# A two-layer block on one core: Du/dt in a stream of its own, new TensorE durations for the planner, products of the identity in the first sample, and a bias loaded earlier

## The chip, the core and the metric

The kernel runs on one core of one Trainium2 chip. Its engines are TensorE (PE: matrix products, with PEld for the loads of their stationary operand), VectorE (DVE), ScalarE (ACT), GpSimd (POOL) and SyncE (SP, which here only issues DMAs). The metric is device time in microseconds; lower is better. Before the change the median of three runs is 2807.39 us (2804.79 to 2811.74).

## What is computed

Sixteen samples of 256 tokens by 256 features, float32 throughout. Each `_L...` is a function of the reference; the indices and masks are left out here.

```python
def reference(x, ...):
    # layer 0
    x = x + attn0(cross(x, fside, embed[itok]))   # softmax(q k^T) v, then causal attention, 16 heads of 16, rotary
    x = x + ffn0(x @ W[cat] + b[cat])             # gate/up/down with FP4-like quantization of inputs and weights
    # layer 1
    du = zX * lap_x(x) + zY * lap_y(x) + zR * x * (1 - x)
    x = x + attn1(rmsnorm(du) * g)                # 16 heads of 64, segments of 128, 16 learned keys in front
    x = x + mixture(conditioned(x))               # 8 experts, top 2, and a shared one
    return x
```

The line `du` (Du/dt in what follows) is three pointwise terms: second differences along both axes, the one along the tokens made as a product with a 256x256 matrix, and a reaction term. attn1 reads nothing else.

## The kernel before

The program has two parts. `woven` does everything up to the second attention, sample by sample, and leaves each sample's x in DRAM; `mixture` then does the experts over all samples. The change touches `woven` alone.

`woven` is written as generators, called streams, each yielding one instruction at a time. `stage_a` loads a sample, does the cross attention, the projection to heads and the row maxima of the first attention's scores; `stage_e` does its exponentials, values and output projection and sets `done["A"]`. `stage_gate`, `stage_up` and `stage_down` quantize and transpose the three weights of the feed forward, once, at the start. `stage_f` is the feed forward (`done["F"]`). `stage_p` loads the constants of the second attention, then for each sample computes Du/dt and its normalized transpose zT (`diffuse`), and the projections of four groups of four heads (`project4`). `stage_g` takes the scores and the softmax of a group (`scores4`), `stage_v` its values and the output projection (`values4`), and after a sample's last group stores x.

`weave` interleaves the streams while the program is built, so that the order on each engine is fixed before anything runs. It keeps a planned time for each engine, from durations that `Unit.cost` gives, and a planned time at which each tile is written and read. In each step it looks at the next instruction of every stream, and issues the one that could start first; ties go to the stream that stands first in the list. A stream that didn't issue the last TensorE instruction is charged `TURN` (0.1 us). A DMA's data counts as there `LANDING` (4.5 us) after its issue. A yielded function is a gate: its stream waits until it returns true. A yielded `Want` asks for a free PSUM buffer; there are two pairs of banks and four single banks (`g.singles`) for all streams.

The engines then run their fixed orders. An instruction that waits holds up all that stands behind it on its engine; SP's DMAs too are issued in order, one after another.

At the start SP issues, in this order: the first sample's xT, fT, the embedding row, fside and x (`fetch_a`), then wqkv, bqkv, three small tables, the output bias `bout`, `wout0`, and the first pieces of the three feed forward weights. GpSimd's first work is x + bout, then the query `a_qT`; TensorE's first products are the scores of the cross attention from `a_qT`, and VectorE's `a_stat` takes their row maxima.

`diffuse` is part of `stage_p`: for sample b it is yielded after the four projections of sample b - 1, and the projections of b come behind it. The tile zT has one buffer. `project4` loads `wq`, `wv` and the rows `wo` of the output projection; `wo` is read by `values4` at the end of the group and has three buffers.

All helpers that record instructions do it in one line (160 before), so groups of the profile are told apart by tiles.

Of the kernel before, what the change touches and what calls it, by code (L numbers as in the profile page):

```python
# [12 lines left out]
F32 = mybir.dt.float32  # L13
# [6 lines left out]
P = 128  # L20
S = 256
D = 256
H = 16
DH0 = 16
DH1 = 64
# [91 lines left out]
class Op:  # L117


    def __init__(self, choices, outs, ins):  # L120
        self.choices, self.outs, self.ins = choices, outs, ins

# [1 line left out]
HOP = 0.15  # L126
LANDING = 4.5
TURN = 0.1


def is_ap(x):
# [3 lines left out]
def row_size(ap):  # L135
    return math.prod(ap.shape[1:])
# [9 lines left out]
class Unit:  # L146
# [17 lines left out]
    def cost(self, fn, outs, ins):  # L164
        if self.name == "SP":
            return 0.06
        if self.name == "PE":
            if fn == "transpose":
                return 0.15
            lhsT, rhs = ins  # L170
            fp32 = 4 if rhs.dtype == F32 else 1
            rows, cols, n = lhsT.shape[0], row_size(lhsT), row_size(rhs)
            side = (2 if rows <= 32 else 1) * (3 if cols <= 32 else 2 if cols <= 64 else 1)
            return max((2 if fp32 == 4 else 1) * cols / 2070, fp32 * n / 2070 / side) + 0.01
        fixed, each = COSTS[self.name]
        n = max(row_size(x) for x in outs[:1] + ins)
        if fn == "reciprocal":
            each = 0.006
        return fixed + each * n + (0.3 if len(outs) > 1 else 0)


def weave(streams):

    free, written, read, rings = {}, {}, {}, {}
    turn = None
    names = lambda aps: [x.tensor.name for x in aps]

    def ready(op, engine):
        t = 0.0
        for n in names(op.ins):
            when, by = written.get(n, (0.0, engine))
            t = max(t, when + (HOP if by != engine else 0.0))
        for x in op.outs:
            n = x.tensor.name
            before = [written.get(n), read.get(n)]
            ring = rings.get(getattr(x.tensor, "tag", None), [])
            if n not in ring and ring:  # L200
                bufs = x.tensor.bufs or x.tensor.tag_meta.bufs
                if len(ring) >= bufs:
                    before += [written.get(ring[-bufs]), read.get(ring[-bufs])]
            for p in before:
                if p and not p[1] == engine == "SP":
                    t = max(t, p[0] + (HOP if p[1] != engine else 0.0))
        return t

    def issue(op, choice, start):
        engine, cost, call = choice  # L210
        free[engine] = start + cost
        end = start + cost + (LANDING if engine == "SP" else 0.0)
        for n in names(op.ins):
            if end > read.get(n, (0.0, engine))[0]:
                read[n] = (end, engine)
        for x in op.outs:
            n, tag = x.tensor.name, getattr(x.tensor, "tag", None)
            written[n] = (end, engine)
            if tag is not None and n not in rings.setdefault(tag, []):
                rings[tag].append(n)  # L220
        call()

    def least(want):

        return min(want.free, key=lambda x: ready(Op([], [x], []), "PE"))


    waiting = [[s, None, None] for s in streams]
    while waiting:
        best, moved = None, False  # L230
        for rank, w in enumerate(waiting):
            while w[1] is None or (callable(w[1]) and w[1]()):
                moved = True
                try:
                    w[1], w[2] = w[0].send(w[2]), None
                except StopIteration:
                    w[0] = None
                    break
            if w[0] is None or callable(w[1]):
                continue  # L240
            if isinstance(w[1], Want):
                if not w[1].free:
                    continue
                op = Op([("PE", 0.0, None)], [least(w[1])], w[1].ins)
            else:
                op = w[1]
            for c in op.choices:
                start = max(ready(op, c[0]), free.get(c[0], 0.0))
                if c[0] == "PE" and w is not turn:
                    start += TURN  # L250
                key = (start, rank, c[1])
                if best is None or key < best[0]:
                    best = (key, w, c, start)
        waiting = [w for w in waiting if w[0] is not None]
        if best is not None:
            _, w, c, start = best
            if isinstance(w[1], Want):
                w[2] = least(w[1])
                w[1].free.remove(w[2])
            else:  # L260
                issue(w[1], c, start)
                if c[0] == "PE":
                    turn = w
            w[1] = None
        else:
            assert moved, "all streams wait"
# [25 lines left out]
def woven(k):  # L292
    nc, tc = k.nc, k.tc
    with ExitStack() as ctx:
        g = Stages()
        g.k, g.a, g.B, g.ident = k, k.a, k.B, k.ident
        g.pe, g.dve, g.act = Unit("PE", nc.tensor), Unit("DVE", nc.vector), Unit("ACT", nc.scalar)
        g.pool, g.sp = Unit("POOL", nc.gpsimd), Unit("SP", nc.sync)
        pool = lambda name, bufs, **kw: ctx.enter_context(tc.tile_pool(name=name, bufs=bufs, **kw))
        g.w = pool("w", 1)  # L300
        g.xp = pool("x", 5)
        g.a_, g.f_, g.l_ = pool("sa", 1), pool("sf", 1), pool("sl", 1)
        space = bass.MemoryType.PSUM
        psum = pool("psum", 1, space=space)
        g.pairs = [psum.tile([P, 2, 512], F32, name=f"pair{i}") for i in range(PAIRS)]
        g.singles = [psum.tile([P, 512], F32, name=f"single{i}") for i in range(8 - 2 * PAIRS)]
        g.live, g.kT = {}, {}
        g.x, g.io, g.done = {}, {}, {"W": 0, "A": 0, "M": 0, "E": 0, "F": 0, "P": 0, "G": 0, "V": 0, "L": 0}
        with tc.manual_schedule():
            weave([stage_a(g), stage_e(g), stage_gate(g), stage_up(g), stage_down(g), stage_f(g), stage_g(g), stage_p(g), stage_v(g)])  # L310


def load(g, pool, name, shape, src):
# [27 lines left out]
def stage_a(g):  # L341
    k, a = g.k, g.a
    yield from fetch_a(g, 0)
    g.wqkv, op = load(g, g.w, "wqkv0", [P, 2, 3 * D], a["w_qkv0"])
    yield op
    g.bqkv, op = load(g, g.w, "bqkv0", [P, 3 * D], a["L0_attn_b_qkv"].unsqueeze(0).to_broadcast([P, 3 * D]))
    yield op
    for name in ("cos0", "sin0", "nsin0"):
        t, op = load(g, g.w, name, [P, 2, DH0 // 2], a[name])
        setattr(g, name, t)  # L350
        yield op
    g.bout, op = load(g, g.w, "bout0", [P, D], a["L0_attn_b_out"].unsqueeze(0).to_broadcast([P, D]))
    yield op
    g.wout0, op = load(g, g.w, "wout0", [P, 2, D], a["w_out0"])
    yield op

# [356 lines left out]
def stage_gate(g):  # L713

    g.gateT = g.w.tile([P, 2, FF0], F32, name="gateT")
    raw = lambda: g.f_.tile([P, 2, D], F32, name="raw", tag="wide", bufs=3)
    yield from quant_rows(g, "L0_ffn_w_gate", g.gateT, raw, None)
    g.done["W"] += 1


def stage_up(g):

    g.upT = g.w.tile([P, 2, FF0], F32, name="upT")
    scratch = scratch_l(g, ("f_pT", "f_pT"), "up")
    yield from quant_rows(g, "L0_ffn_w_up", g.upT, lambda: tile_l(g, [P, 2, D], "f_v", 3), scratch)
    g.done["W"] += 1
# [71 lines left out]
def stage_p(g):  # L798
    k, a = g.k, g.a
# [48 lines left out]
        g.keys.append(t)  # L848
    g.mhalf = g.w.tile([P, 2], F32, name="mhalf")
    yield g.pool.memset(g.mhalf, -0.5)  # L850
    for b in range(g.B):
        yield lambda b=b: g.done["F"] > b
        zT = yield from diffuse(g, b)
        for n in range(4):
            yield lambda i=4 * b + n: i < g.done["V"] + 3
            g.live[4 * b + n] = yield from project4(g, n, zT)
            g.done["P"] += 1


def diffuse(g, b):  # L860
# [21 lines left out]
    yield g.pool.tensor_tensor(ms, ms, g.mhalf, ALU.pow)  # L882
    for st in range(2):
        yield g.dve.tensor_scalar(u[:, st, :], u[:, st, :], ms[:, st : st + 1], None, ALU.mult)
    zT = tile_l(g, [P, 2, S], "e_zT")
    one = yield from single(g, u)
    pt = one.rearrange("p (c t) -> p c t", c=2)
    for c in range(2):
# [8 lines left out]
def project4(g, n, zT):  # L897

    a = g.a
    wq = tile_l(g, [P, 2, 2, 2 * P], "wq", 2)  # L900
    for which in range(2):
        cols = slice((8 * which + 2 * n) * P, (8 * which + 2 * n + 2) * P)
        yield g.sp.dma_start(out=wq[:, which], in_=a["w_qk1"][:, :, cols])
    wv, wo = tile_l(g, [P, 2, 4 * DH1], "wv", 2), tile_l(g, [P, 2, D], "wo", 3)
    yield g.sp.dma_start(out=wv, in_=a["w_v1"][:, :, n * 4 * DH1 : (n + 1) * 4 * DH1])
    yield g.sp.dma_start(out=wo, in_=a["w_out1"][:, 2 * n : 2 * n + 2, :])
    q = tile_l(g, [P, 2, S], "f_q", 3)
    by_seg = lambda t: t.rearrange("p (s t) -> p s t", s=2)
    for which in range(2):
# [16 lines left out]
        yield from mm_(g, pv[:, st, :], [(zT[:, c, st * P : (st + 1) * P], wv[:, c, :]) for c in range(2)])  # L926
    yield copy_(g, v, pv)
    g.singles.append(one)
    return q, v, wo

# [19 lines left out]
            g.done["L"] = b + 1  # L952


def scores4(g, n, q, v, wo):

    keys = g.keys[n]
    prob = tile_l(g, [P, 2, 4, PM + P], "f_prob", 2)
    if n % 2 == 0:
        g.pm = tile_l(g, [P, 2, 8, PM], "f_pm", 2)  # L960
# [566 lines left out]
```

## Time and profile before

| | us |
|---|---|
| median of three runs | 2807.39 |
| the profiled execution | 2814.07 |
| its span | 2812.4 |
| TensorE busy | 2700.6 |
| VectorE busy | 1440.4 |
| ScalarE busy | 927.8 |
| GpSimd busy | 874.7 |
| TensorE's first product starts | 19.53 |
| last part (`mixture`) begins, about | 1820 |

The times of engines are from one execution, taken by the hardware profiler; durations of single instructions come from it too. Its own time, 2814.07 us, is what its span is held against. In the list of groups a line reads: source line, engine, operation, output<-inputs by tile name, partitions x elements and count, then the busy time in us and the mean of one in ns, then the idle time of the engine just before these instructions with what ended it. A product of two float32 operands appears as two records. Matmuls overlap, so the mean of one is longer than busy time divided by count. "PEclk" is the clock that TensorE was granted, as a share of full speed. A table by stretch gives for each: its length, then the busy time and number of instructions of PE, PEld, DVE, ACT and POOL, then PEclk, the share of DMA and its GB/s.

### The profile page before, as it was taken

What the parts mean: (1) busy time and instruction counts of PE and PEld (TensorE: products, weight loads), DVE (VectorE), ACT (ScalarE), POOL (GpSimd) and SP (SyncE); (2) the same over time, 40 slices, a digit from 0 to 9 for tenths busy, and PEclk for the clock granted to TensorE, in tenths of its full rate; (3) what the DMA queues carried; (4) which work ended last, traced back from release to release, by engine and by line L of the source; (5) the groups of instructions that cost most, each with busy time, mean ns of one, the idle gap of its engine ahead of it and who ended that gap; (6) DMA issues with size and microseconds to landing.
All of it is one profiled execution on the core that took longest, in us unless ns stands there. A gap on an engine that the chain in (4) does not pass through costs nothing. (4 is left out here: it accounts for less than half of the span.)

```text
span 2812.4 us, 41924 instructions
## 1 busy us (share of the span) xinstructions
PE 2700.6 (96%) x15819; PEld 2034.8 (72%) x15819; DVE 1440.4 (51%) x3117; ACT 927.8 (33%) x2414; POOL 874.7 (31%) x1030
## 2 busy tenths in 40 slices
PE   5899999999999999999999998799999999999999
PEld 3667777777777777777777777655566888888866
DVE  6456766776776776776777666424340000000023
ACT  2223433334333334334434333323322222222221
POOL 4333433434434444444444343322330000000035
PEclk7789999999999999999999999899999999999999
DMA  3122221222222221231231232241112355555523
GB/s 112 57 83 76 66 84 38 93 79 64 91 90 63 87 94 55 90 96 59 88 97 39 79 94 68 65 141 46 51 38 77 126 189 196 197 197 196 197 83 105
DMA packets 196525, 270.38 MB, mean 96 GB/s; under 512 B 34912, under 2 KB 167264, under 8 KB 186976
## 3 DMA queue, kind: packets, MB, share of 16 engines
q1 hardware_dynamic: 190176, 250.87, 28.0%
q0 software_dynamic: 6144, 16.79, 2.0%
q8 instruction: 127, 2.08, 0.3%
q14 instruction: 78, 0.64, 0.1%
HBM read 207.05 MB, written 60.56 MB: 95 GB/s over the span
## 5 line engine op out<-in xcount | busy, mean ns | idle before, releaser
L160 ACT ACTIVATE f_prob<-pair,f_stat 128x144 f32<-128x144 f32 x512 | 191.2, 379 | 274.1 <-DVE f_stat L160 266.4
L160 DVE TENSOR_TENSOR pair<-pair,mask 128x256 f32<-128x256 f32 (+1 forms) x384 | 198.8, 518 | 132.9 <-PE pair L160 91.9
L1166 POOL DMA_INDIRECT got<-osort,pos_o x64 | 62.2, 972 | 628.2 <-PE bank L49 585.7
L160 PE MATMUL single<-e_zT,wq 128*128 128x256 f32 x1024 | 251.5, 389 | 2.8 <-DMA wq<-in_w_qk 1.4
L1148 ACT ACTIVATE ehT<-bank,own_b 128x256 f32<-128x256 f32 x280 | 132.9, 475 | 348.7 <-PE bank L49 348.7
L49 PE MATMUL bank<-ysT,w 128*128 128x256 f32 x1120 | 247.5, 379 | 0.2 <-ACT ysT L113 0.2
L49 PE MATMUL bank<-w,ehT 128*128 128x256 f32 x1120 | 247.5, 379 | 0.0
L49 PEld LDWEIGHTS bank<-ysT,w 128*128 128x128 f32 x1120 | 212.7, 190 | 29.4 <-ACT ysT L113 0.5
L49 PEld LDWEIGHTS bank<-w,ehT 128*128 128x128 f32 x1120 | 210.2, 190 | 27.2
L160 PEld LDWEIGHTS single<-e_zT,wq 128*128 128x128 f32 x1024 | 188.7, 192 | 39.0 <-DVE pair L160 3.3
L160 PE MATMUL pair<-keys,f_q 32*128 32x144 f32 x2048 | 162.0, 297 | 0.0
L160 PEld LDWEIGHTS pair<-keys,f_q 32*128 32x128 f32 x2048 | 134.2, 187 | 35.8 <-issue 25.2
L160 POOL TENSOR_TENSOR f_q<-f_t,f_t 128x256 f32<-128x256 f32 x128 | 91.6, 736 | 205.6 <-DVE f_t L160 201.0
L160 DVE TENSOR_TENSOR x<-x,single 128x512 f32<-128x512 f32 (+1 forms) x112 | 67.8, 605 | 161.6 <-PE single L160 157.0
L160 POOL TENSOR_SCALAR_AFFINE_SELECT b_e<-b_e 128x512 f32<-128x512 f32 x128 | 83.2, 650 | 207.0 <-ACT b_e L160 206.4
L160 ACT ACTIVATE b_e<-pair 128x768 f32<-128x768 f32 x128 | 103.7, 811 | 132.7 <-PE pair L160 106.1
L160 POOL TENSOR_TENSOR keys<-f_t,f_t 128x256 f32<-128x256 f32 x128 | 93.2, 741 | 167.5 <-DVE f_t L160 166.4
L1156 DVE TENSOR_TENSOR eo<-bank,eb 128x512 f32<-128x512 f32 x35 | 24.2, 692 | 234.4 <-PE bank L49 234.4
L160 PE MATMUL single<-wo,f_oT 128*128 128x256 f32 x512 | 131.6, 390 | 9.1 <-ACT f_oT L160 7.5
L160 DVE TENSOR_REDUCE qpad<-pair 128x2 f32<-128x256 f32 (+1 forms) x256 | 131.0, 554 | 4.4
L160 PE MATMUL pair<-b_qS,b_qkT 17*128 17x256 f32 (+1 forms) x1024 | 123.3, 363 | 5.7 <-DVE qpad L160 2.3
L160 PE MATMUL pair<-b_qkT 16*128 16x128 f32 (+1 forms) x1024 | 126.8, 368 | 1.9 <-ACT b_qkT L160 1.6
(289 smaller groups left out, 5238.5 us busy)
## 6 DMA issues: line engine op xcount, KB each, us to landing
w<-in_w SPq DMA_DIRECT2D x70, 1024.0 KB
ysort<-zero SPq DMA_DIRECT2D x32, 1024.0 KB
wq<-in_w_qk SPq DMA_DIRECT2D x128, 256.0 KB
wv<-in_w_v SPq DMA_DIRECT2D x64, 256.0 KB
wo<-in_w_out SPq DMA_DIRECT2D x64, 256.0 KB
ys<-ysort SPq DMA_DIRECT2D x35, 256.0 KB
osort<-eo SPq DMA_DIRECT2D x35, 256.0 KB
eb<-in_b SPq DMA_DIRECT2D x35, 128.0 KB
```

Of the source, the lines that this page charges most:

```text
L49: nc.tensor.matmul(out, lhsT, rhs, start=start and i == 0, stop=stop and i == last)
L160: return Op([(self.name, self.cost(fn, outs, aps), lambda: call(*args, **kw))], outs, aps)
L1148: nc.scalar.activation(hT[:, f, :], ph, AF.Gelu_apprx_tanh, bias=b1[:, f : f + 1])
L1156: nc.vector.tensor_tensor(o, po, b2.unsqueeze(1).to_broadcast([P, 2, D]), ALU.add)
L1166: nc.gpsimd.indirect_dma_start(out=g, out_offset=None, in_=k.osort[:, :], in_offset=bass.IndirectOffsetOnAxis(ap=r.pos_o[:, i, t : t + 1], ...
```

## The change

It has four parts.

1. `bout` is loaded right behind the first sample's x, ahead of wqkv.
2. The durations that the planner has for TensorE are replaced.
3. A stream `stage_fill` issues products of the identity with itself, 128x128, into a single bank that it keeps for the purpose, until the first sample's attention is done. Nobody reads them. The planner adds `GAP` (0.6 us) to their start when it compares, so that one is taken only where no stream could start anything within 0.6 us of it.
4. `diffuse` moves from `stage_p` to a stream of its own, `stage_d`, which may be a sample ahead of the projections: it starts sample b once its feed forward is done and the projections of b - 2 are recorded. zT gets two buffers. `wo` is loaded in `scores4` instead of `project4`, with two buffers instead of three.

```diff
@@ the planner
+GAP = 0.6
...
             if fn == "transpose":
-                return 0.15
+                return 0.12
             lhsT, rhs = ins
-            fp32 = 4 if rhs.dtype == F32 else 1
-            rows, cols, n = lhsT.shape[0], row_size(lhsT), row_size(rhs)
-            side = (2 if rows <= 32 else 1) * (3 if cols <= 32 else 2 if cols <= 64 else 1)
-            return max((2 if fp32 == 4 else 1) * cols / 2070, fp32 * n / 2070 / side) + 0.01
+            rows, cols, t = lhsT.shape[0], row_size(lhsT), row_size(rhs) / 570
+
+            if rows <= 64:
+                return max(0.155 if rows <= 32 else 0.19, t / 2)
+            return max(t / 3.5, 0.08) if cols <= 32 else max(t / 2, 0.13) if cols <= 64 else t
...
-                key = (start, rank, c[1])
+                key = (start + (GAP if op.filler else 0.0), rank, c[1])
...
-                if c[0] == "PE":
+                if c[0] == "PE" and not w[1].filler:
                     turn = w
@@ woven
-            weave([stage_a(g), stage_e(g), stage_gate(g), stage_up(g), stage_down(g), stage_f(g), stage_g(g), stage_p(g), stage_v(g)])
+            weave([stage_a(g), stage_e(g), stage_gate(g), stage_up(g), stage_down(g), stage_f(g), stage_g(g), stage_p(g), stage_d(g), stage_v(g), stage_fill(g)])
+
+
+def stage_fill(g):
+
+
+    one = g.singles.pop()
+    while g.done["A"] < 1:
+        op = g.pe.matmul(one[:, :P], g.ident, g.ident, start=True, stop=True)
+        op.filler = True
+        yield op
+    g.singles.append(one)
@@ stage_a
     yield from fetch_a(g, 0)
+    g.bout, op = load(g, g.w, "bout0", [P, D], a["L0_attn_b_out"].unsqueeze(0).to_broadcast([P, D]))
+    yield op
     g.wqkv, op = load(g, g.w, "wqkv0", [P, 2, 3 * D], a["w_qkv0"])
...
-    g.bout, op = load(g, g.w, "bout0", [P, D], a["L0_attn_b_out"].unsqueeze(0).to_broadcast([P, D]))
-    yield op
@@ stage_p and stage_d
+    g.done["Z"] = 1
     for b in range(g.B):
-        yield lambda b=b: g.done["F"] > b
-        zT = yield from diffuse(g, b)
+        yield lambda b=b: g.done["D"] > b
+        zT = g.zT.pop(b)
...
+def stage_d(g):
+
+    yield lambda: g.done["Z"]
+    for b in range(g.B):
+        yield lambda b=b: g.done["F"] > b and g.done["P"] >= 4 * b - 4
+        g.zT[b] = yield from diffuse(g, b)
+        g.done["D"] = b + 1
@@ diffuse, project4, scores4
-    zT = tile_l(g, [P, 2, S], "e_zT")
+    zT = tile_l(g, [P, 2, S], "e_zT", 2)
...
-    wv, wo = tile_l(g, [P, 2, 4 * DH1], "wv", 2), tile_l(g, [P, 2, D], "wo", 3)
+    wv = tile_l(g, [P, 2, 4 * DH1], "wv", 2)
...
-    yield g.sp.dma_start(out=wo, in_=a["w_out1"][:, 2 * n : 2 * n + 2, :])
...
-def scores4(g, n, q, v, wo):
+def scores4(g, n, q, v):
...
+    wo = tile_l(g, [P, 2, D], "wo", 2)
+    yield g.sp.dma_start(out=wo, in_=g.a["w_out1"][:, 2 * n : 2 * n + 2, :])
```

Apart from the 90 products of the identity that the planner finds room for, each engine has the same work as before; only ScalarE and VectorE share the copies out of PSUM differently, since the planner picks the one that is free first.

More of the change, by code (lines that the diff above doesn't have):

```diff
@@ L121, in __init__ @@
         self.choices, self.outs, self.ins = choices, outs, ins
+        self.filler = False
 COSTS = {"DVE": (0.15, 0.00105), "ACT": (0.16, 0.00083), "POOL": (0.30, 0.0016)}
@@ L306, in woven @@
         g.singles = [psum.tile([P, 512], F32, name=f"single{i}") for i in range(8 - 2 * PAIRS)]
+        g.zT = {}
         g.live, g.kT = {}, {}
-        g.x, g.io, g.done = {}, {}, {"W": 0, "A": 0, "M": 0, "E": 0, "F": 0, "P": 0, "G": 0, "V": 0, "L": 0}
+        g.x, g.io, g.done = {}, {}, {"W": 0, "D": 0, "Z": 0, "A": 0, "M": 0, "E": 0, "F": 0, "P": 0, "G": 0, "V": 0, "L": 0}
         with tc.manual_schedule():
-            weave([stage_a(g), stage_e(g), stage_gate(g), stage_up(g), stage_down(g), stage_f(g), stage_g(g), stage_p(g), stage_v(g)])
+            weave([stage_a(g), stage_e(g), stage_gate(g), stage_up(g), stage_down(g), stage_f(g), stage_g(g), stage_p(g), stage_d(g), stage_v(g), stage_fill(g)])
[6 more added lines that the diff above has]
+    g.singles.append(one)
 def load(g, pool, name, shape, src):
@@ L928, in project4 @@
     g.singles.append(one)
-    return q, v, wo
+    return q, v
 def stage_g(g):
```

## The prediction

> **What bounds the kernel now.** I read the page first (busy shares, the slices of the span), then a table by stage, then TensorE's timeline at the two ends of the first part, where the table shows it standing.
>
> ```profile
> span 2812.4 us, 41924 instructions
> PE 2700.6 (96%) x15819; PEld 2034.8 (72%) x15819; DVE 1440.4 (51%) x3117; ACT 927.8 (33%) x2414; POOL 874.7 (31%) x1030
> PE   5899999999999999999999998799999999999999
> PEclk7789999999999999999999999899999999999999
> ```
>
> TensorE (PE) is busy nearly everywhere, and its clock is below full in the first slices and once after slice 25. The table says how much that is; after the stretch come its length, each engine's busy time, the granted clock and DMA.
>
> ```profile
> 18.00:47.00 29.00, 18.27 (x62) 11.93 (x64) 24.89 (x48) 9.14 (x22) 18.87 (x22) 0.88 0.52 159
> 47.00:98.00 51.00, 47.87 (x240) 31.78 (x238) 29.70 (x65) 15.97 (x34) 18.07 (x25) 0.50 0.04 9
> 98.00:140.00 42.00, 34.67 (x179) 23.96 (x180) 22.96 (x45) 10.51 (x19) 14.21 (x30) 0.87 0.28 86
> 140.00:300.00 160.00, 149.44 (x886) 105.67 (x882) 99.31 (x199) 49.00 (x126) 53.44 (x64) 0.87 0.24 76
> 300.00:1500.00 1200.00, 1183.73 (x8350) 897.26 (x8346) 873.46 (x1753) 460.46 (x1342) 501.01 (x584) 0.99 0.25 77
> 1500.00:1820.00 320.00, 296.19 (x2069) 231.65 (x2068) 201.23 (x398) 117.11 (x396) 118.89 (x141) 0.98 0.22 69
> 1820.00:2812.00 992.00, 970.45 (x4047) 732.55 (x4047) 188.33 (x610) 264.30 (x475) 144.88 (x151) 0.99 0.41 132
> ```
>
> From 300 to 1500 us TensorE stands only 1200 - 1183.73 = 16.3 us: little can be won there. The part after 1820 us is the mixture, whose code is unchanged. What can move is (a) the first sample, where TensorE waits 19.5 us for its first product and then works 51 us at a clock of 0.50 though busy 47.87 of them, and (b) 1500 to 1820 us, with 23.8 us standing.
>
> **The sum is made against** the profiled execution, 2814.07 us with a span of 2812.4. It lies 6.7 us (0.24%) above the median of the three runs, 2807.39; I apply the difference to the median.
>
> **Part 1, the bias loaded early: -0.4 us.** The chain at the start (first column: start, second: length):
>
> ```profile
> 17.00 1.26 POOL L160 TENSOR_TENSOR x<-x,bout 128x512 f32<-128x512 f32 x1 [11.91 <-DMA bout<-in_L_attn_b_out]
> 18.08 0.69 DVE L160 TENSOR_REDUCE q_amax<-raw 128x32 f32<-128x512 f32 x1 [12.68 <-DMA raw<-in_L_ffn_w_gate]
> 19.53 3.78 PE L160 MATMUL pair<-fT,a_qT 128*128 128x256 f32 x8 [19.53 <-POOL a_qT L160]
> 23.35 0.69 DVE L160 TENSOR_REDUCE a_stat<-pair 128x2 f32<-128x512 f32 x1
> ```
>
> The DMA of the bias was issued at 11.60 and its reader started at 17.00, 5.4 us on. It moves on SP's queue past wqkv, bqkv and three small tables, to just behind x (issued 7.12 for 0.47), so about 7.6; with the same 5.4 us POOL starts at 13.0, and two POOL steps of 1.26 bring the scores to 15.5 instead of 19.53: 4 us. But the reader of the scores is VectorE's a_stat, and in VectorE's order, the same in the changed kernel up to there, ten instructions of weight quantization stand before it. They start at 18.08 when the gate's weights land, and run without a gap to 23.35. The bytes queued before those weights are the same. So the 4 us end in front of a_stat. What goes is that q_unit (0.72) and q_unit_up (0.59) ran slower beside POOL than the same shape later (0.32 at 29.96); I take 0.4 of it. Ends: 0 and -4.0. The five DMAs passed land 0.4 us later by issue time; wqkv is read at 33.9, bqkv at 36.8: hidden.
>
> **Part 2, products of the identity: -3 us, the part with the wide bounds.** The changed program's order holds 90: 26 ahead of the first scores, 11 behind them, 2 in small waits, 14 where it waits for qpad, 37 more until sample 0's attention is done. Their price is not in the trace. The nearest rows at full clock:
>
> ```profile
> L160 PE MATMUL single<-e_zT,wq 128*128 128x256 f32 x712 | 174.2, 388 | 1.3 <-DMA wq<-in_w_qk 1.2
> L160 PE MATMUL single<-ident,f_prob 128*128 128x128 f32 x360 | 53.3, 276 | 2.3 <-ACT f_pT L160 2.3
> ```
>
> A product of two f32 operands leaves two records (512 in the order, 1024 on the page). Half of a 256-wide product is 174.2/712 = 0.245; two records at a transpose's 53.3/360 = 0.148 are 0.30. I take 0.27, and 0.5 at half clock (two transposes there are 0.5).
> - The 26 start when the identity is made (1.5 us), at 0.5 end by 14.5, before the scores at 15.5. The 11 follow the scores (19.3), end by 24.8; TensorE's next work waits for POOL until 27.2. Both free, with 1.0 and 2.4 us to spare; if the cover is gone, up to 13 and 5.5.
> - The 14 stand in a wait of 3.15 us plus a step: 14 x 0.27 = 3.8 against 3.4: +0.4; at half clock +3.6.
> - The 37 stand in TensorE's queue from 45 to 105 us, where only 5.5 us of waits are left. At half clock they cost 37 x 0.5 = 18.5, less 5.5: +13. At full clock the 54.8 us of work there halve to 27.4, the products take 10, and some 8 of waits remain (an estimate from the 5.5): 45 instead of 60, about -14.
>
> So the clock decides. The trace: at 47.2 it falls after a stretch whose only work was transposes and 16-row products, and stays at 0.50 to 98.4 with TensorE busy 47.87 of 51 us. It rose at 33.6, 98.4 and 153.0, each time behind 3.4 us and more of 128-row products 256 wide. [...] By the row, busy is not enough; the kind of work counts, 51 us of it did not release anything. The row decides: a group of 7 products (3.5 us) may release it, [...] and the first groups after the 14 are 1, 1 and 4 within some 6 us. I take clock held at both ends of the stretch and lost in the middle: rather nearer the middle of -14 and +13 (0), with 3 us for the cross attention of sample 1 (83 to 98 us), which has a group of 6 behind its first products and can release the clock sooner. -3; both ends kept.
>
> **Part 3, Du/dt in its own stream: -6 us.** It has the same instructions; zT has two buffers, wo is loaded where the scores begin, with two buffers instead of three. In mid-run TensorE never waits for it. At the end:
>
> ```profile
> 1617.09 0.81 PE L160 MATMUL single<-ident,e_u 128*128 128x128 f32 x4 [1.21 <-DVE e_u L160]
> 1690.62 1.99 PE L160 MATMUL single<-wo,f_oT 128*128 128x256 f32 x8 [1.45 <-DVE f_oT L160]
> 1694.95 0.70 PE L160 MATMUL single<-e_zT,wq 128*128 128x256 f32 x2 [0.56 <-ACT e_zT L160]
> 1696.06 1.56 PE L160 MATMUL single<-e_zT,wq 128*128 128x256 f32 x6 [0.41 <-ACT e_zT L160]
> 1700.10 0.66 PE L160 MATMUL single<-ident,f_prob 128*128 128x128 f32 x4 [2.48 <-POOL f_prob L160]
> ```
>
> These are the Du/dt of samples 13 and 14, each in line before its projections. By TensorE's order its transposes for sample 14 come 640 products before the first part ends instead of 432, for sample 15 444 instead of 244: a whole sample's projections ahead. The five waits sum to 6.1; I take 6. Ends: 0 (the softmax's chain is late next) and -10 (sample 15's feed forward also ends 496 instead of 564 products before the end, so less of the tail runs without other work). The wo load now waits, on SP, for values two groups back; behind it stand the next wq and wv. It is issued some 10 us before its reader; if not hidden, a few us at the last samples.
>
> **Part 4, durations: 0.** They only reorder. Summing both formulas over one sample's products gives the planner's price, 113 before and 102 now; the trace has about 107 (1183.73 x 64/712). So the plan was 5% above the chip and is 5% below: other engines get less lead. Ends: -5 and +16 (the idle of the middle doubles).
>
> Sum: -0.4 - 3 - 6 = -9.4; on the profiled time 2804.7, on the median 2798.
>
> **Rivals.**
> - *The clock is held through the whole first sample*: -0.4 - 14 - 6 = -20: 2787. For it: in the middle the clock mostly stays at 1.00 with only a third of some windows in wide products. Against: 47 to 98 us.
> - *The identity products are in the way (slower)*: the clock falls within the first 6 us after qpad, then all 37 cost 0.5 and those of the 14 that overrun too: +13 + 3.6 - 0.4 - 6 = +10: 2818. It decides from the point where the clock is 0.5 before the group of 7 and that group doesn't release it. For it: the clock of 0.50 with a busy engine.
> - *Thin plan*: the stream of 300 to 1500 us stalls for 16 us more: -9.4 + 16: 2814. Against: VectorE is busy 73% there and has room.
> - *The bias moves the start* by the full 4 us (VectorE's order would have to run earlier): inside the range.
>
> **How the numbers follow.** Forecast 42% (2798, own range 2791 to 2805), clock held 22%, in the way 24%, thin plan 12%. This kernel's runs tell apart about 0.3%, 8.4 us: faster is below 2799, slower above 2815.8. Faster: a little over half of the forecast and the clock held, 0.46; slower: most of the third case and a share of the fourth, 0.22; within, 0.32. Range 2784 to 2819.
>
> **What would show it.** Scores start near 15.5 but a_stat at 23 (part 1); the clock between 45 and 100 us, and wout of sample 0 ending before or after 105.4 (part 2); no waits on e_u or e_zT after 1600 us less the shift (part 3); idle in the middle near 16 us (part 4). A first sample faster at a clock of 0.5, or a middle that loses more than 16 us, makes it wrong.

## The result and the profile after

The changed kernel takes 2793.78 us (median of five runs, 2789.39 to 2794.98) where the kernel before takes 2809.38 (2804.79 to 2811.74): a ratio of 0.9937, 95% interval 0.9924 to 0.995. (This ratio is not the quotient of the two medians, which is 0.9944; here and below the two differ by up to 0.001.) Both run anew later, beside other kernels, gave 2790.67 against 2811.87: 0.9915, interval 0.9893 to 0.9937. The profiled execution after took 2794.98 us, with a span of 2793.3; the one before took 2814.07.

From the page of after, its span, TensorE's slices of the span and the clock granted in them:

```profile
span 2793.3 us, 42335 instructions
...
PE   7999999999999999999999999799999999999999
...
PEclk7879999999999999999999999899999999999999
```

The digits look nearly as before. The table by stretch (columns as before: length, busy time of PE, PEld, DVE, ACT and POOL, then PEclk, DMA share, GB/s) shows more:

```profile
18.00:47.00 29.00, 22.77 (x114) 17.28 (x112) 25.85 (x50) 8.01 (x20) 16.12 (x19) 0.87 0.51 164
47.00:98.00 51.00, 48.36 (x314) 37.02 (x316) 29.91 (x66) 16.58 (x35) 19.10 (x26) 0.70 0.05 16
98.00:140.00 42.00, 36.64 (x208) 24.76 (x206) 22.30 (x45) 11.21 (x20) 15.07 (x31) 0.89 0.26 77
140.00:300.00 160.00, 149.43 (x864) 104.77 (x864) 100.86 (x200) 48.71 (x116) 53.32 (x66) 0.86 0.21 68
300.00:1500.00 1200.00, 1177.49 (x8364) 893.90 (x8364) 867.89 (x1749) 470.72 (x1370) 483.35 (x583) 1.00 0.25 79
1500.00:1820.00 320.00, 295.37 (x2074) 231.12 (x2073) 200.53 (x401) 116.95 (x387) 121.61 (x155) 0.97 0.26 80
1820.00:2793.00 973.00, 963.17 (x4029) 728.31 (x4027) 186.26 (x602) 260.90 (x472) 141.15 (x136) 1.00 0.40 131
```

The clock from 47 to 98 us rose from 0.50 to 0.70. In 300 to 1500 us TensorE now stands 22.5 us (1200 - 1177.49) instead of 16.3. But a table by fixed times compares different work. So I also laid the two executions side by side by work done: each product of `woven` counted at its full-clock time from the trace (products of the identity at nothing), and the time read off at the same amount of work. This count is only a ruler: its 1300 units from 420 to 1720 took 1131 us. The four columns are the first sample, the next four or so, the middle, and the end:

| us of time for the work | first 60 units of work | 60 to 420 | 420 to 1720 | 1720 to the end | end of `woven`'s products |
|---|---|---|---|---|---|
| before | 113.8 | 355.7 | 1131.3 | 218.7 | 1819.5 |
| after | 113.7 | 350.1 | 1133.4 | 202.8 | 1800.0 |
| difference | 0 | -6 | +2 | -16 | -19.5 |

Most of the gain is in the last stretch. Counted instead by the lengths of the products' records, which overlap, the four differences are -2, -1, -2 and -15: the last column stands with either ruler, and the others are too small to be told from nothing in one pair of executions. The two rows of the table by stretch for just that part, before and then after:

```profile
1600.80:1819.50 218.70, 196.70 (x1349) 156.61 (x1347) 129.71 (x254) 80.01 (x290) 84.06 (x99) 0.98 0.22 68
```

```profile
1597.10:1799.90 202.80, 192.76 (x1337) 156.23 (x1335) 126.14 (x247) 76.29 (x277) 77.80 (x92) 0.98 0.24 75
```

TensorE stood 22.0 us there (218.7 - 196.7) and now stands 10.0. From the lists of its waits (who waits, for whom, total us, times, longest), first, three of 1600 to 1820 us of before, then the longest of 1597 to 1800 us of after:

```profile
PE single L160 <- POOL f_prob L160: 11.6, 7, 5.1
PE single L160 <- DVE e_u L160: 1.2, 1, 1.2
PE single L160 <- ACT e_zT L160: 1.0, 2, 0.6
```

```profile
PE single L162 <- POOL f_prob L162: 5.5, 2, 5.1
PE single L162 <- ACT f_pT L162: 1.1, 4, 0.4
PE single L162 <- POOL c_y L162: 1.1, 1, 1.1
PE single L162 <- ACT f_oT L162: 1.1, 2, 0.7
```

No wait on e_u or e_zT, the tiles of Du/dt, remains; but half of what went, 6.1 us, is waits on f_prob, the tile of the softmax. One wait of 5.1 us on the softmax of the last group stands in both kernels: nothing is behind it to be done.

At the start, from the timeline of after:

```profile
14.73 1.26 POOL L162 TENSOR_TENSOR x<-x,bout 128x512 f32<-128x512 f32 x1 [9.66 <-DMA bout<-in_L_attn_b_out]
17.27 3.78 PE L162 MATMUL pair<-fT,a_qT 128*128 128x256 f32 x8 [8.09 <-POOL a_qT L162]
19.09 0.69 DVE L162 TENSOR_REDUCE q_amax<-raw 128x32 f32<-128x512 f32 x1 [13.72 <-DMA raw<-in_L_ffn_w_gate]
23.79 0.68 DVE L162 TENSOR_REDUCE a_stat<-pair 128x2 f32<-128x512 f32 x1
```

The scores start 2.3 us earlier than before, and their reader a_stat 0.4 us later (23.35 before).

### The profile page after: what moved, and what is told of

It is laid out like the page before. It is cut to its first block, busy times and chain, and to the rows that moved or that the text cites. A ratio compares the mean times of both kernels' runs of the same rounds, so it can differ in the third digit from the quotient of the medians.

```text
span 2793.3 us, 42335 instructions
## 1 busy us (share of the span) xinstructions
PE 2701.6 (97%) x15999; PEld 2045.2 (73%) x15999; DVE 1434.2 (51%) x3113; ACT 934.3 (33%) x2418; POOL 856.5 (31%) x1030
## 5 line engine op out<-in xcount | busy, mean ns | idle before, releaser
L162 POOL TENSOR_SCALAR_AFFINE_SELECT b_e<-b_e 128x512 f32<-128x512 f32 x128 | 83.1, 649 | 216.8 <-ACT b_e L162 216.1
L162 POOL TENSOR_TENSOR f_prob<-f_prob,f_stat 128x1024 f32<-128x1024 f32 x64 | 125.8, 1965 | 0.0
```

The source lines that it names most:

```text
L162: return Op([(self.name, self.cost(fn, outs, aps), lambda: call(*args, **kw))], outs, aps)
```

## The experiments

The changed kernel has four parts. The first four runs took parts away or put one in alone.

**Du/dt in its own stream, alone.** The kernel before with parts of the diff that concern `stage_d`, zT and `wo`; nothing else.

```diff
+    g.done["Z"] = 1
...
-        yield lambda b=b: g.done["F"] > b
-        zT = yield from diffuse(g, b)
+        yield lambda b=b: g.done["D"] > b
+        zT = g.zT.pop(b)
...
+def stage_d(g):
...
+        yield lambda b=b: g.done["F"] > b and g.done["P"] >= 4 * b - 4
```

> Only the stream for Du/dt (with zT doubled and wo moved), old durations, no products of the identity, the bias late. Du/dt theory: the gain lies between 1600 and 1820 us and is this part alone, so 2796 us (10 to 14 below before), with no waits for e_u, e_zT or the f_oT behind it near the end. Clock theory (the identity products made the gain): 2809, as before. Durations theory: 2809, the tail as before.

**Everything but that stream.** The changed kernel with `diffuse` back in `stage_p`, and zT and `wo` buffered and loaded as before; of its edit:

```diff
-        yield lambda b=b: g.done["D"] > b
-        zT = g.zT.pop(b)
+        yield lambda b=b: g.done["F"] > b
+        zT = yield from diffuse(g, b)
```

> The change without the stream for Du/dt. Du/dt theory: the gain is gone but for some 4 us, 2803 to 2807. Clock theory and durations theory: 2794, as the whole change.

**Everything but the products of the identity.**

```diff
-            weave([..., stage_d(g), stage_v(g), stage_fill(g)])
+            weave([..., stage_d(g), stage_v(g)])
```

> The change without the products of the identity. Du/dt theory: 2794 with 3 us either way; the clock between 47 and 98 us back near 0.5, but sample 0's attention ends within 3 us of 103.5 all the same, since the room that the faster clock makes is what the products fill. Clock theory: 2805 or more, sample 0's attention 10 us later.

**The whole change, but Du/dt not a sample ahead.**

```diff
-        yield lambda b=b: g.done["F"] > b and g.done["P"] >= 4 * b - 4
+        yield lambda b=b: g.done["F"] > b and g.done["P"] >= 4 * b
```

> The change, but Du/dt of sample b may start only once the projections of b - 1 are recorded, as before. If the gain comes from Du/dt being a sample ahead: 2803 to 2807. If the stream of its own or the later load of wo is enough: 2794.

Measured together, with the kernel before at 2813.42 us:

| kernel | median us | ratio to before, 95% |
|---|---|---|
| own stream alone | 2913.22 | 1.0355 (1.0336 to 1.0374) |
| without the own stream | 2865.22 | 1.0177 (1.0153 to 1.0201) |
| without the identity products | 2796.27 | 0.9942 (0.9924 to 0.996) |
| no look-ahead | 2872.2 | 1.0208 (1.0185 to 1.0231) |

Three of the four expectations fell, and by far: the own stream alone costs 100 us, and the change without it costs 52. The third held in its time, 2796.27; sample 0's attention there ended at 106.9 us, 0.4 outside what was expected. The parts do not add. By work done, the loss lies in the middle: 1251.1 us for the work from 420 to 1720 with the own stream alone, 1179.6 without it, 1186.4 without the look-ahead, where before takes 1131.3.

What differs there is the order. Compared sample by sample, TensorE's order as the planner wrote it comes to repeat exactly: in the kernel before from sample 6 on, one sample like the last, 104.4 us each. With the own stream alone it repeats too, but another order, of 116.1 us. Without the look-ahead it repeats with a period of three samples (94, 98 and 142 us). Without the own stream it repeats only near the end. In the whole change, and without the identity products, it repeats at 104.5 us. What the bad order costs is in the rows of one sample, first of the kernel with the own stream alone (116 us), then of before (104 us):

```profile
732.00:848.00 116.00, 109.17 (x734) 82.05 (x733) 76.47 (x147) 43.08 (x125) 44.04 (x51) 0.96 0.23 71
```

```profile
656.00:760.00 104.00, 102.91 (x732) 78.24 (x730) 76.12 (x154) 39.81 (x117) 43.67 (x51) 1.00 0.25 79
```

TensorE stands 6.8 us instead of 1.1, and its clock is 0.96: three spells of some 3.4 us at half clock in this sample. Together that is, as an estimate from the two rows and the three spells, about 11 us (5.7 of standing, and half of the 10.2 at half clock) of the 12 that the sample takes longer. The waits over this sample and the one ahead of it (616 to 848 us) of the kernel with the own stream alone, and one of the spells on its timeline:

```profile
PE single L160 <- DVE e_u L160: 3.7, 2, 1.8
PE single L160 <- POOL d_h L160: 3.1, 2, 1.5
PE pair L160 <- issue: 2.6, 2, 1.3
PE single L160 <- ACT f_pT L160: 2.0, 6, 0.4
```

```profile
747.68 0.82 PE L160 MATMUL pair<-b_qS,b_qkT 17*128 17x256 f32 x8
750.03 1.12 PE L160 MATMUL single<-ident,d_h 128*128 128x128 f32 x4 [1.53 <-POOL d_h L160]
750.94 2.97 PE L160 MATMUL single<-e_zT,wq 128*128 128x256 f32 x8
753.84 0.92 PE L160 MATMUL pair<-b_qkT 16*128 16x128 f32 x8
```

The projections at 750.94 (eight records, so four products) take 2.97 us; eight such records take 1.99 at full clock (at 688.02 us of before). As I read it, the wait of 1.53 us is paid a second time in the clock, which fell at 749.7 us, while TensorE waited, and stayed at 0.50 to 753.1. The next run tests whether it is the order in the middle that costs, or the stream.

**The stream ahead in the tail only.** The kernel before with the own stream, ahead of its projections for samples 13 to 15 alone. The edit is against the kernel with the own stream alone.

```diff
-        yield lambda b=b: g.done["F"] > b and g.done["P"] >= 4 * b - 4
+        yield lambda b=b: g.done["F"] > b and g.done["P"] >= 4 * b - (4 if b >= 13 else 0)
```

> Kernel before with Du/dt in its own stream, but ahead by a sample only for samples 13 to 15; TensorE's order is then that of before up to there, and the tail has Du/dt early. Nothing else of the change is in it. Theory A (the gain of the stream is in the tail, and the loss of the stream alone, +99 us, came from the other repeating order that it led to in the middle): samples 104.4 us apart as before, no wait on e_zT after 1600 us, 2799 to 2804 where before is 2813 (-9 to -14). Rival B (the stream itself costs, some 12 us in each sample in which it runs ahead): three such samples, +20 to +40.

Measured: 2812.13 us against 2813.24, ratio 0.9998 (0.9986 to 1.0009). Rival B is out: nothing like 20 us was lost. The middle, where the stream isn't ahead, took 1133.7 us for the work of 1131.3 before, and the last stretch, where it is, took 216.1 us, 2.6 less than before. But theory A's gain didn't come either. The waits on Du/dt were gone; those on f_prob were 11.6 us in all, as before. From its timeline:

```profile
1708.51 3.72 PE L160 MATMUL single<-e_zT,wq 128*128 128x256 f32 x16
1716.48 0.66 PE L160 MATMUL single<-ident,f_prob 128*128 128x128 f32 x4 [4.25 <-POOL f_prob L160]
```

TensorE waits 4.25 us for the softmax of a group that it had once reached later: as I read it, an early Du/dt moves other work forward and leaves less to do beside the softmax. This is the case that the prediction kept as its lower end, "0 (the softmax's chain is late next)". (The profiled execution, 2801.26 us, was the fastest of 14; its granted clock, 0.979, was also the highest of them, 0.971 to 0.979.)

**One price closer to the trace.**

```diff
             if fn == "transpose":
-                return 0.12
+                return 0.15
```

> Kernel after with one number of the planner changed: a transpose is priced 0.15 us instead of 0.12, closer to the 0.148 of the trace of before. Theory A (what counts is which repeating order the greedy planner falls into, not how true a price is): its order in the middle repeats with a lag between feed forward and Du/dt as in the stream-alone kernel, so about 116 us a sample, 2880 to 2910. Rival C (truer durations give the better plan): 2785 to 2797, samples 104 us apart.

Measured: 2823.33 us, ratio 1.0037 (1.0024 to 1.0051), some 30 above the change. The samples of the middle are 107.4 us apart. Both expectations missed: rival C's is out, and theory A's direction held but its size did not, 107.4 and not 116; the lag that I read the number from doesn't name the order. That a truer price makes the kernel slower holds for this one price.

**The own stream and the durations together**, without identity products and with the bias late.

> Kernel before with Du/dt in its own stream and the new durations; no products of the identity, and the bias late. TensorE's order is that of the change without the products. Theory A: these two together are the change, 0.994 of before as in the run without the products (2796 where before is 2813), samples 104.5 us apart. Rival D (the early bias gives its 4 us): 0.9955 or more, 2800.

Measured: 2795.95 us, ratio 0.9937 (0.9922 to 0.9953). As theory A has it: these two parts, of which the one alone costs 100 us and the other, with the small parts, 52, gain 17 together. Its last stretch took 201.5 us.

**The bias late**, measured twice, the second time beside the changed kernel anew.

```diff
-    g.bout, op = load(g, g.w, "bout0", [P, D], a["L0_attn_b_out"].unsqueeze(0).to_broadcast([P, D]))
-    yield op
     g.wqkv, op = load(g, g.w, "wqkv0", [P, 2, 3 * D], a["w_qkv0"])
...
+    g.bout, op = load(g, g.w, "bout0", [P, D], a["L0_attn_b_out"].unsqueeze(0).to_broadcast([P, D]))
+    yield op
     g.wout0, op = load(g, g.w, "wout0", [P, 2, D], a["w_out0"])
```

> Kernel after with the bias of the attention loaded late as before; TensorE's order is that of after. My sum: 0 to 0.4 us behind after, 2794 to 2795 where before is 2811 (ratio 0.9937 or 0.9938). Rival D (the first scores' 4 us count): 2798.

It took 2786.38 us, ratio 0.9905 (0.9885 to 0.9924): faster than any theory had it. So it was run again beside the change.

> The changed kernel itself, beside the same with the bias late. The bias was loaded late in a run that came out 7 us below the change (2786 against 2794), while both took the same time at the same granted clock (2793 at 0.977). Theory A (the bias does nothing; each execution draws how the first sample's clock falls): 2786 to 2795, within 3 us of the late one when both have been run anew, and 1.9 us less for each 0.001 of granted clock. Rival B (with the bias early the scores at 17.3 us end a busy spell early, and the clock falls at a worse place): 5 to 9 us above the late one again.

> The kernel with the bias late once more. Theory A: within 3 us of the change run beside it. Rival B: 5 to 9 us below it, its granted clock at 0.980 to 0.983 in most executions and that of the change at 0.977 to 0.980.

Measured together: the change 2790.67 us (2786.69 to 2794.6), the bias late 2788.57 (2782.82 to 2795.06), ratios 0.9915 (0.9893 to 0.9937) and 0.9907 (0.9884 to 0.9931). That is theory A's range and not rival B's. (In their profiled executions the clock was 0.87 from 18 to 47 us and 0.83 from 47 to 98 us with the bias early, 0.81 and 0.87 with it late.) Over all their runs here and in the result (11 and 12) the medians are 2792.2 and 2788.0: no measurement shows a gain from the early bias, and some 4 us against it can't be excluded.

**More products of the identity.** On the kernel with the bias late, first with a smaller `GAP`, then also up to the fourth sample.

```diff
-GAP = 0.6
+GAP = 0.3
```

> Bias late, and the products of the identity offered for waits of 0.3 us and more instead of 0.6: 119 instead of 90, all in the first sample; TensorE's order from sample 5 on and in the tail as in the change. Theory A (more of them hold the clock in the first sample): the first sample ends at 95 us or earlier, 0 to 4 us below the kernel with 90. Rival C (they are in the way): 29 more at 0.25 to 0.5 us, up to 7 to 14 us above it.

Measured: 2789.76 us, ratio 0.9918 (0.9896 to 0.9939): no gain beside the 2788.57 with 90 and no 7 us of loss. The first sample ended at 98.1 us, as with 90 (97.2).

```diff
-GAP = 0.6
+GAP = 0.3
...
-    while g.done["A"] < 1:
+    while g.done["A"] < 4:
```

> As the run with 119, and the products are offered until the attention of four samples is done: 191, over the first 350 us; the order from sample 6 on and in the tail as in the change. The trace of the kernel with 90 has half clock in 57 us between 113 and 308 us. Theory A (products in the small waits keep the clock there too): half of it goes, 10 to 15 us below the kernel with 90, 2772 to 2777. Rival C (in the way: in these samples TensorE stands for only 10 us in 160, so they come on top): 0 to 15 us above it, clock no higher than 0.90 in 140 to 300 us.

Measured: 2776.21 us (2776.05 to 2781.34), ratio 0.9873 (0.9849 to 0.9896). All its runs lie below all runs of the change measured beside it: this is the fastest version, 14 us better than the change and 12 better than the same with 90 products. Two rows of the table by stretch show it, first with 90 products (the second run with the bias late), then with 191:

```profile
98.00:140.00 42.00, 37.95 (x203) 25.34 (x203) 25.51 (x50) 11.93 (x21) 15.75 (x32) 0.81 0.14 47
140.00:300.00 160.00, 148.95 (x891) 105.15 (x890) 101.82 (x204) 50.32 (x121) 55.16 (x68) 0.89 0.22 68
```

```profile
98.00:140.00 42.00, 40.37 (x271) 30.13 (x270) 27.24 (x55) 13.14 (x25) 17.04 (x33) 1.00 0.09 26
140.00:300.00 160.00, 156.89 (x1079) 116.92 (x1078) 113.06 (x230) 56.57 (x149) 61.91 (x77) 1.00 0.26 81
```

With the clock held at 1.00, VectorE too does 11% more in 140 to 300 us (113.06 against 101.82): all of the first samples run faster. How it comes about shows in the same place of the two timelines, with 90 and with 191:

```profile
126.64 0.82 PE L162 MATMUL pair<-b_qS,b_qkT 17*128 17x256 f32 x8
128.63 0.33 PE L162 MATMUL single<-ident,qpad 128*128 128x128 f32 x1 [1.17 <-DVE qpad L162]
...
131.83 1.51 PE L162 MATMUL single<-b_e,vpad 128*32 128x256 f32 x16
133.27 1.65 PE L162 MATMUL pair<-b_qkT 16*128 16x128 f32 x8
```

```profile
122.70 0.92 PE L162 MATMUL pair<-b_qS,b_qkT 17*128 17x256 f32 x8
123.49 0.92 PE L162 MATMUL pair<-b_qkT 16*128 16x128 f32 x8
124.34 1.60 PE L162 MATMUL single<-ident 128*128 128x128 f32 x12
125.79 0.38 PE L162 MATMUL single<-ident,qpad 128*128 128x128 f32 x2
```

With 90, a wait of 1.17 us for qpad stands open, and from 131.3 us, between two and three microseconds on, the clock is at 0.50: the eight records of 16-row products take 1.65 us instead of 0.92. With 191, six products of the identity (twelve records) stand in such a wait and the clock stays at 1.00. The expectation's rival took TensorE's 10 us of standing for all that the products could hide in; as I read it, it left out that at full clock the same work leaves more waits to fill: the 72 more that stand behind the first sample take some 17 us (an estimate, 72 x 0.235 us, the price of one in the trace of after), and TensorE's standing from 98 to 300 us fell by 10.4 (15.1 to 4.7).

## Why the prediction was right, and where it was not

The time, 2793.78, lies 4 us below the forecast of 2798, in its own range, and the change is faster by more than the 0.3% that the prediction took its runs to tell apart. The forecast was a change of -9.4; between the medians measured together it is -15.6, between the profiled executions -19.1. So the time lies well within the range although the largest term of the sum was too small by far. By its own steps:

- **Part 1, the bias (-0.4; ends 0 and -4.0).** Right in that it gains nothing. The scores start at 17.27, not 15.5: the bias took 6.9 us from issue to landing, not 5.4. But as the step says, a_stat stands behind VectorE's quantization, which starts at 19.09, and the gain ends there: the scores end at 21.05, and a_stat starts at 23.79. Of the 0.4 that the step counted on: q_unit took 0.18 us with GpSimd idle where it had taken 0.72 beside it, and q_unit_up, beside it in both, 0.59 in both; but the quantization started 1.0 us later than before. Kernels with the bias early and late, measured together, came some 2 us apart, the early one behind.
- **Part 2, the identity products (-3; -14 to +13).** That the clock decides was right, the size uncertain. In the profiled execution they brought 2 us or less by the end of the first sample: the clock was 0.70 from 47 to 98 us, the 54.6 us of half clock in the spells that begin between 47 and 105 us became 30.7, and the products filled what that freed (attention done at 103.5 instead of 105.6 us). Over runs they brought more. The cleanest pair is two kernels measured together, alike but for the products, both with the bias late: 2795.95 us without and 2786.38 with 90, so 9.6. Over all, the kernels with 90 have ratios of 0.9937, 0.9915, 0.9905 and 0.9907, those without 0.9942 and 0.9937, a mean difference of 0.0024 or about 7 us, with intervals of about 0.002 either way on each. The price of one at full clock was 3.29/14 = 0.235 us where I took 0.27. The prediction's hinge, that "a group of 7 products (3.5 us) may release" the clock, was my estimate from the trace of before, and it came out both ways: in the profiled execution of the result the seven at 60.5 us did not, and half clock lasted to 79.9; in the second profiled execution of the same kernel the clock rose at 66.4 us, behind the same seven at 62.4, and was 0.83 from 47 to 98 us. So executions of one and the same kernel differ in just this. What the prediction did not ask is whether smaller groups keep it: in the run with 191, offered for waits of 0.3 us and more, they did, at 1.00 from 98 to 300 us, where it was 0.81 (to 140 us) and 0.89 (from there) with 90.
- **Part 3, the own stream (-6; 0 to -10).** The term was mis-sized: -16 in the last stretch, outside its own ends. The sum counted five waits, 6.1 us; of the 11.6 us of waits on f_prob it had one of 2.48, and 6.1 of them went. TensorE's standing there fell by 12, and its busy time by 4, part of that because the last half-clock spell before the end is 3.4 us shorter (6.8 instead of 10.2). And the gain is not the stream's alone. The run with the stream ahead in the tail has -2.6, the one with it everywhere but the old durations took 207.5 us (-11), the executions of kernels with both, with or without products of the identity, 199.9 to 204.6, the one without the stream 215.0 (another ruler moves these by up to 5 us). As I read it, "a whole sample's projections ahead" does the work only in an order that also leaves something beside the softmax.
- **Part 4, the durations (0; -5 to +16).** Right in size as a term of this sum, wrong as a statement about durations. "They only reorder" is true, and reordering is worth up to 100 us here: the stream with the old durations loses 100, with the new ones it gains 17, and one price altered by 0.03 us costs 30. The end of +16 came from the plan being 5% short; no such average tells which repeating order the greedy rule falls into. The prediction read TensorE's order at both ends of `woven` and priced the middle by an average. (Its own 1183.73 x 64/712 is 106.4 and not 107, which changes nothing.) Read over one sample of the middle, the order would have shown that another one repeats there, from sample 6 on, whose cost no row of the profile of before gives; that it came out at 104.5 us a sample against 104.4 was luck as far as the sum goes.

The rival *clock held* (2787) didn't happen as put, the clock being 0.70 and not full in the profiled stretch, and 0.83 in the second profiled execution of the change; some executions came near its time. *In the way* is out, though its condition came true in the profiled execution, where the clock had fallen at 59.4 us, ahead of the group of 7 at 60.5, and the group didn't release it: its 10 us of loss did not come, no kernel with the products was slower than its like without, and with 191 the gain is largest. *Thin plan*: the middle stood 6.2 us more, not 16.

What stays open: why the planner falls into the one order or the other. That it does, and what it costs, is shown; a rule that would tell it from the durations was not found, and the one I tried for the transposes gave the wrong size. Nor were the new durations tried alone; the kernel without the stream had the other two parts as well.

## What to carry to other kernels

Where a planner or scheduler writes the order, the parts of a change can't be priced one by one: a part that loses 100 us alone can be half of what wins, so compare the whole program's order over a full period of the loop, and measure parts only with the order held. A wait can be paid twice, once standing and once in the clock behind it: here one of 1.53 us, and then 2.97 us instead of 1.99 for the projections behind it. Filler work can then pay where the engine is nearly busy already and the clock wavers: here, offered over four samples instead of one and for shorter waits, it brought 12 us more. And before a few microseconds are put down to an edit, look at the granted clock of each run: here 0.001 of it went with 1.9 us.

## What the hardware showed beyond that

- **The spread of runs goes with the clock.** Over 43 runs of the kernel before, time and mean granted clock go together: 1.9 us less for each 0.001 (correlation -0.87; 0.971 to 0.980, 2805 to 2824 us). The change and its twin with the bias late take the same time at the same clock (2793.2 and 2793.6 us of span at 0.977); what differs is how often each was drawn.
- **When it fell and rose.** The half-clock spells in the traces of before and after last multiples of about 3.4 us (3.4, 6.8, 10.2, 13.7, 17.1, 20.5, and 51.2 in the first sample of before). Most begin behind waits among small products: in the trace of before, TensorE was busy for at most 72% of the 3.4 us ahead of each fall. But one came without a wait. In the trace of after the clock fell at 83.34 us behind 3.4 us without a gap, filled mostly with products of 16 or 17 rows and products of 32 columns; the two steps:

```profile
79.93:83.34 3.41, 3.41 (x43) 2.25 (x44) 2.12 (x4) 1.57 (x4) 1.60 (x2) 1.00 0.02 5
83.34:86.75 3.41, 3.41 (x12) 2.90 (x13) 2.13 (x5) 0.90 (x3) 1.50 (x2) 0.50 0.00 0
```

Nor did being busy end a spell: in the kernel with own stream and durations alone, without identity products, TensorE was busy 47.54 of 51 us from 47 to 98 at a clock of 0.53. In the trace of before there are products of 128 rows, 256 or more wide, in the 3.4 us ahead of each rise. Products of the identity, 128 wide, stood ahead of a rise too: in the kernel with 191 a spell ended behind a step that held sixteen of their records and two of a transpose:

```profile
57.34:60.75 3.41, 3.41 (x18) 3.41 (x18) 3.27 (x7) 0.35 (x2) 1.58 (x3) 0.50 0.00 0
60.75:64.16 3.41, 3.12 (x30) 2.71 (x28) 3.16 (x9) 1.15 (x2) 1.90 (x3) 1.00 0.00 0
```

So in these traces the busy time of the profile alone doesn't tell when the clock falls or rises: 3.41 of 3.41 us stood ahead of a fall, and 47.54 of 51 went by at 0.53. As I read it, the kind of product counts in both directions; no run here varied rows and columns one at a time, so which property it is isn't settled.
